# A scan with experts on one core: the copies of a triangular solve at six places, and a transposing matmul three pairs behind its gram

## The chip, the cores and the metric

The kernel runs on one core of one Trainium2 chip. Its metric is the device time of one execution in microseconds (us), the median of several runs. A core has five engines that each work through a queue of their own: TensorE (PE) for matmuls, VectorE (DVE), ScalarE (ACT) and GpSimd (POOL) for elementwise work, and SyncE (SP), which here issues every DMA. PEld is TensorE's weight load.

## The reference, cut to what matters

```python
x = L0_attn_x                                   # (8, 1024, 256)
xn = _layernorm(x, axis=-1)
v = xn @ Wkv[256:].T + bkv[256:]
def step(W, inp):                               # scan over the 1024 time steps
    xt, vt = inp                                # 8 rows, one of each sequence
    y = xt @ W.T
    gW = 2 / (8 * 256) * ((y - vt).T @ xt)
    return W - eta * gW, y
s = scan(step, W0, (xn, v))
probs = softmax(xn @ router_w.T + router_b)     # 16 experts, the best 6, renormalized
ffn = sum over e of (xn @ expert_w[e]) * gate[:, e]   # divided by the gates' sum, plus a tiny term
out = x + s * silu(ffn)
```

The scan is a recurrence: the weight W is corrected after each time step by the error that it made on that step. All else is independent from row to row.

## The kernel before

**Tiles.** The 1024 steps are cut into 64 tiles of 16 steps; a tile has 16 x 8 = 128 rows. Inside a tile the recurrence becomes a triangular system: with A made of the products of the tile's rows with one another (gram), the errors of all 128 rows are the solution of (1 + A) e = p, where p is the error under the W of the tile's start. The kernel inverts the triangle ahead of time, for a batch of tiles at once, and then multiplies. Batches have 1, 1, 2, 4, 4, 4 tiles and then eight each; the batches of eight begin with tiles 16, 24, 32, 40, 48 and 56.

**One tile's steps.** The load of x (L110, on SP), layernorm (L200: bn_stats L204, bn_aggr L206 into mv, xn), a round trip through DRAM that turns xn (bounce L228, xT L230), and the cast of xT into a high and a low part, xT_two (`split`, L151 to L153: ScalarE casts the high part, DVE or POOL subtracts the low one). `products` (L263): two matmuls make gram in PSUM (L268), and ScalarE casts gram's second half, the cross terms, into cross (L274). `products_end` (L276): one matmul against the identity adds cross transposed onto gram (L278), and DVE makes xx (L283) and the masked a (L284). `project` (L286): vr, the values and router logits, from which DVE makes lg and hv. `errors_1` (L524): pe = x W, and p = 2 hv + pe (L534), split into p_hi and p_lo. `errors_2` (L541): the solution e by three matmuls with u_hi and u_lo, from which ScalarE makes step_hi (L546) and DVE step_lo (L548) and hy (L552). `update` (L554): six matmuls add the step to W (wt_ps), and wt_hi and wt_lo are cast from it. `experts` (L566): eight pairs of experts, six matmuls of 128x512 each into h (three PSUM buffers); the parts are scaled by the gates and summed on ScalarE (part, L583), POOL (mix, L586) and DVE (mix, L592 and L594). `finish` (L599): m (L604), th (L606), my (L608, L610, L611) and the output's DMA (L612).

**The solve of a batch** goes through solve_0 to solve_6, on blocks of 32 rows: solve_1 and solve_2 invert the diagonal blocks (q2, then uq at L424, and its transposed form tq at L444). At its end solve_2 copies the four blocks of uq into u_full and the four of tq into t_half, eight copies on ScalarE for a batch of eight (L448, L451). solve_3 makes z (L467 and around), solve_4 y, which is copied into u_full and t_half (L483, L485), solve_5 z2 from u_full (L492, L500), solve_6 y2 from t_half and z2 (L505), and then splits u_full into u_hi and u_lo (L517).

**What sets the order.** PE's and SP's order is the order in which the program text issues the work: `put(slot, pair, what)` (L647) files each step under a tile and a pair of its experts, and the loop at the end (L707 to L715) issues, for each tile and pair, first the steps filed there and then that pair of experts. So one pair of experts, six matmuls of h, is the unit in which steps are placed, eight to a tile. With f the first pair of a batch of eight, its solve_1 to solve_6 stand at f-11, f-9, ... f-1 (L670). Gram of tile i stands at pair 8(i-9)+1 in the long run (L676), products_end one pair later, load 21 pairs ahead of gram, layernorm 10 and transpose_x 1 ahead. The order on ScalarE, DVE and POOL is not written out; a scheduler sets it when the kernel is built, by the text's order as priority and by when it reckons that an instruction's inputs are ready. Gram and vr share two PSUM buffers ("misc").

Of the kernel before, what the change touches and what calls it, by code (L numbers as in the profile page):

```python
# [36 lines left out]
P = 128  # L37
Q = 32
# [5 lines left out]
GROUP = 4  # L44
BATCH = 8
AHEAD = 5
FAR = 9
# [6 lines left out]
def ttt_moe_kernel(  # L54
# [12 lines left out]
    nc = tc.nc  # L67
# [30 lines left out]
    batches = [1, 1, 2, 4, 4, 4]  # L98
# [92 lines left out]
    def at(b, size=Q):  # L191
        return slice(b * size, (b + 1) * size)
# [221 lines left out]
    def step_q(g, name, rhs, out):  # L414

        c = g.count
        ps = solving(f"{name}_ps_{g.n}")
        for j in range(c):
            for b in range(P // Q):
                nc.tensor.matmul(  # L420
                    ps[at(b), j * Q : (j + 1) * Q], lhsT=gram_of(g.first + j)[at(b), 0, at(b)],
                    rhs=rhs[at(b), j, :], start=True, stop=True, skip_group_check=True,
                )
        nc.vector.tensor_add(  # L424
            out, ps[:, : c * Q].rearrange("p (j q) -> p j q", q=Q),
            ident_q.unsqueeze(1).broadcast_to([P, c, Q]),
        )
# [13 lines left out]
    def solve_2(g):  # L441
        c = g.count
        step_q(g, "uq", g.q2, g.uq)
        nc.vector.transpose(  # L444
            g.tq.rearrange("p j q -> p (j q)"), g.uq.rearrange("p j q -> p (j q)")
        )
        for b in range(P // Q):
            nc.scalar.copy(g.u[at(b), :, at(b)], g.uq[at(b)])  # L448
        for odd, js, ms in g.halves:
            for b in range(2):  # L450
                nc.scalar.copy(g.t[at(2 * odd + b), ms, at(b)], g.tq[at(b), js])  # L451

    def solve_3(g):
        c = g.count
# [47 lines left out]
    def solve_6(g):  # L502
# [15 lines left out]
        for j in range(g.count):  # L518
            tiles[g.first + j].u_hi, tiles[g.first + j].u_lo = u_hi[:, j, :], u_lo[:, j, :]

    solve = [solve_1, solve_2, solve_3, solve_4, solve_5, solve_6]


# [93 lines left out]
    opened, started = {}, {}  # L617
# [22 lines left out]

    def solve_x(n, m):
        solve[m](started[n])


    events = {}

    def put(slot, pair, what, *args):  # L647
        events.setdefault((slot, pair), []).append((what, args))
# [19 lines left out]
    for n, c in enumerate(batches):  # L668
        f = 8 * sum(batches[:n])
        spots = solves.get(n, [f - 11 + 2 * m if c > GROUP else f - 10 + 2 * m for m in range(len(solve))])  # L670
        for m, spot in enumerate(spots):
            put(spot // 8, spot % 8, solve_x, n, m)
    preps = {1: 6, 2: 10, 3: 12, 4: 17, 5: 19, 6: 25, 7: 27, 8: 33, 9: 35, 10: 41, 11: 49}
    for i in range(1, NT):
        near = preps.get(i, 8 * (i - AHEAD) + 1)
        spot = preps.get(i, 8 * (i - FAR) + 1)  # L676
        if 11 < i < 23:
            spot = 49 + (i - 11) * 16 // 3
        norm, turn = {1: (1, 4), 2: (7, 9), 3: (8, 8)}.get(i, (spot - 10, spot - 1))
        fetch = max(4, spot - 21)  # L680
        apart = max(turn, 8 * (i - 2) + 6)
        if i >= BY_PE:
            put(fetch // 8, fetch % 8, load, i)
        put(norm // 8, norm % 8, layernorm, i)
        put(turn // 8, turn % 8, transpose_x, i)
        put(apart // 8, apart % 8, split_x, i)
        put(spot // 8, spot % 8, products_x, i)
        put(near // 8, near % 8, project_x, i)
        put((spot + 1) // 8, (spot + 1) % 8, products_y, i)

    ctx.enter_context(tc.manual_schedule(engines={mybir.EngineType.PE, mybir.EngineType.SP}))

# [54 lines left out]
```

## Time and profile before

| what | us |
|---|---|
| median of 3 runs | 1000.82 |
| the three runs | 1002.66, 998.97, 1000.82 |
| the profiled execution's own time | 1001.66 |
| its span, from the first to the last instruction | 999.6 |
| PE busy | 965.9 |
| DVE busy | 763.0 |
| ACT busy | 427.6 |
| POOL busy | 442.1 |

The span is what the hardware profiler saw of one execution; some 2 us of that execution's own time lie around it. Busy times are sums over the span. The rows of groups name the line, the engine, the operation, what is written and read, and the mean time of one; "idle before" is the time in which the engine stood still just ahead of such an instruction, with the instruction that ended most of it. The granted clock of TensorE was 0.997 of full speed. In the plain tiles, the time from the first matmul of a tile's experts to that of the next tile is 14.06 us, and one pair of experts takes 1.4 to 1.6 us of PE.

### The profile page before, as it was taken

The page shows a single profiled execution, that of the slowest core. Times are in us where ns is not written, and L with a number is a line of the kernel's source. Part 1 is how long each engine was busy: PE and PEld are TensorE (multiplying, and loading weights), DVE is VectorE, ACT ScalarE, POOL GpSimd, SP SyncE. Part 2 cuts the span into 40 slices and gives each one's busy share as a digit, 9 for nine tenths or more (in the row PEclk, how much of TensorE's full clock was granted, in tenths as well). Part 3 has the DMA queues.
Part 4 walks back from the last instruction along what each step waited for, and adds up shares of the span by engine and source line. Part 5 has one row for each costly group of instructions (what it writes and reads, how often), then busy time and mean ns, then how long its engine had stood idle before and what let it go on. Part 6 is the DMA issues. An engine that isn't in the chain of part 4 may idle for free.

```text
span 999.6 us, 19616 instructions
## 1 busy us (share of the span) xinstructions
PE 965.9 (97%) x6672; PEld 796.4 (80%) x6672; DVE 763.0 (76%) x2207; ACT 427.6 (43%) x1101; POOL 442.1 (44%) x675
## 2 busy tenths in 40 slices
PE   5999999999999999999999999999999999999997
PEld 4778778878778887888878888788887888888885
DVE  6988696877868878787777878679786787757665
ACT  6654454453443334433344343543335333443332
POOL 6543444444444453444434454344443544343443
PEclk9999999999999999999999999999999999999999
DMA  8111111111111111111110111111110110000000
GB/s 237 30 53 33 48 38 54 42 44 50 26 40 34 34 43 31 36 43 37 27 44 22 43 44 39 27 39 26 42 44 22 43 43 22 8 11 11 11 11 11
DMA packets 67092, 38.66 MB, mean 39 GB/s; under 512 B 38176, under 2 KB 66992, under 8 KB 66992
## 3 DMA queue, kind: packets, MB, share of 16 engines
q1 hardware_dynamic: 66992, 37.41, 13.9%
q8 instruction: 53, 0.87, 0.4%
q14 instruction: 47, 0.39, 0.1%
HBM read 21.13 MB, written 16.25 MB: 37 GB/s over the span
## 4 chain that ended last, share of the span: by engine, by line
PE 53%; DVE 21%; DMA 8%; issue 5%; POOL 5%; ACT 5%; SPq 3%; POOLq 0%; DVEq 0%; ACTq 0%
PE h L259 41%; DVE mix L594 5%; DMA x<-in_L_attn_x_dram 5%; PE pe L259 4%; PE vr L259 3%; ACT part L583 3%; PE wt_ps L259 2%; POOL mix L586 2%; DVE q L433 2%; DMA bounce<-xr 1%; DVE mix L592 1%; DVE wt_lo L153 1%; SPq L230 1%; POOL rstd L210 1%; DMA raw<-in_L_ffn_expert_w_dram 1%
## 5 line engine op out<-in xcount | busy, mean ns | idle before, releaser
L259 PE MATMUL h<-we,xT_two 128*128 128x512 f32 x3072 | 779.7, 399 | 3.7 <-ACT part L583 3.2
L259 PEld LDWEIGHTS h<-we,xT_two 128*128 128x128 f32 x3072 | 554.5, 189 | 119.2 <-ACT part L583 5.8
L594 DVE SCALAR_TENSOR_TENSOR mix<-h,gate,mix 128x256 f32<-128x256 f32 x576 | 265.6, 475 | 87.8 <-PE h L259 52.7
L583 ACT ACTIVATE part<-h,gate 128x256 f32<-128x256 f32 x384 | 182.0, 475 | 315.8 <-DVE mix L594 177.2
L586 POOL TENSOR_TENSOR mix<-mix,part 128x256 f32<-128x256 f32 x256 | 189.6, 741 | 156.6 <-ACT part L583 152.6
L608 POOL TENSOR_TENSOR my<-m,hy 128x256 f32<-128x256 f32 x64 | 47.5, 742 | 167.7 <-DVE m L604 159.9
L611 POOL TENSOR_TENSOR my<-my,x 128x256 f32<-128x256 f32 x63 | 46.5, 738 | 73.1 <-DVE top L387 25.9
L586 POOL TENSOR_TENSOR mix<-part,part 128x256 f32<-128x256 f32 x64 | 48.3, 754 | 50.8 <-ACT part L583 50.8
L152 ACT CAST p_hi<-p 128x256 fp32r<-128x256 f32 x64 | 26.0, 406 | 90.6 <-DVE p L534 90.3
L153 DVE TENSOR_TENSOR wt_lo<-wt_ps,wt_hi 128x512 fp32r<-128x512 f32 x64 | 43.0, 672 | 23.6 <-ACT wt_hi L152 23.6
L259 PE MATMUL vr<-w_vr,xT_two 128*128 128x272 f32 x384 | 60.0, 292 | 0.0
L259 PEld LDWEIGHTS vr<-w_vr,xT_two 128*128 128x128 f32 x384 | 55.7, 191 | 4.3
L204 DVE BATCH_NORM_STATS2 st<-x 128x6 f32<-128x256 f32 x64 | 26.9, 422 | 41.0 <-DMA x<-in_L_attn_x_dram 41.0
L153 POOL TENSOR_TENSOR xn_lo<-xn,xn_hi 128x256 fp32r<-128x256 f32 x64 | 47.7, 746 | 6.5 <-ACT xn_hi L152 6.4
L208 POOL TENSOR_SCALAR ve<-mv 128x1 f32<-128x1 f32 x64 | 15.1, 238 | 78.7 <-DVE mv L206 66.6
L546 ACT ACTIVATE step_hi<-pe,neg_c 128x256 fp32r<-128x256 f32 x64 | 30.3, 474 | 37.0 <-PE pe L259 37.0
L217 DVE TENSOR_SCALAR xn<-x,mv,rstd 128x256 f32<-128x256 f32 x40 | 32.8, 819 | 15.6 <-POOL rstd L210 15.2
L153 DVE TENSOR_TENSOR p_lo<-p,p_hi 128x256 fp32r<-128x256 f32 x64 | 42.5, 664 | 2.5 <-ACT p_hi L152 1.1
L259 PEld LDWEIGHTS pe<-wt_hi,xT_two 128*128 128x128 f32 x256 | 39.0, 188 | 6.0 <-ACT wt_hi L152 0.4
L152 ACT CAST xT_two<-xT 128x256 fp32r<-128x256 f32 x60 | 24.3, 406 | 44.4 <-PE h L259 23.9
L259 PE MATMUL pe<-wt_hi,xT_two 128*128 128x256 f32 x256 | 40.8, 281 | 0.0
L548 DVE SCALAR_TENSOR_TENSOR step_lo<-pe,neg_c,step_hi 128x256 fp32r<-128x256 f32 x64 | 30.4, 475 | 13.5 <-ACT step_hi L546 13.5
(117 smaller groups left out, 1182.8 us busy)
## 6 DMA issues: line engine op xcount, KB each, us to landing
x<-in_L_attn_x_dram SPq DMA_DIRECT2D x64, 128.0 KB, 2.7
out_dram<-my SPq DMA_DIRECT2D x64, 128.0 KB, 2.3
bounce<-xr SPq DMA_DIRECT2D x60, 128.0 KB, 2.3
xT<-bounce SPq DMA_DIRECT2D x240, 32.0 KB, 1.8
raw<-in_L_ffn_expert_w_dram SPq DMA_DIRECT2D x16, 256.0 KB, 6.1
w_raw<-in_L_attn_Wkv_dram SPq DMA_DIRECT2D x1, 256.0 KB, 2.8
w_raw<-in_L_attn_W_dram SPq DMA_DIRECT2D x1, 256.0 KB, 5.6
bias<-in_L_attn_bkv_dram SPq DMA_DIRECT2D x1, 128.0 KB, 4.8
```

Source lines behind the costliest of these rows:

```text
L152: nc.scalar.copy(hi, src)
L153: (engine or nc.vector).tensor_sub(lo, src, hi.bitcast(F32))
L204: nc.vector.bn_stats(st, xt)
L217: nc.vector.tensor_scalar(q.xn, xt, mv[:, 0:1], rstd, ALU.subtract, ALU.mult)
L259: nc.tensor.matmul(o, lhsT=a, rhs=b, start=first and m == 0, stop=(m == len(terms) - 1), **kw)
L546: nc.scalar.mul(q.step_hi, e, neg_c)
L548: nc.vector.scalar_tensor_tensor(q.step_lo, e, neg_c, q.step_hi.bitcast(F32), op0=ALU.mult, op1=ALU.subtract)
L583: nc.scalar.mul(part, he, gate)
L586: nc.gpsimd.tensor_add(new, q.mix[1], part)
L594: nc.vector.scalar_tensor_tensor(new, he, gate, q.mix[j], op0=ALU.mult, op1=ALU.add)
L608: nc.gpsimd.tensor_mul(my, m, q.hy)
L611: (nc.vector if i == NT - 1 else nc.gpsimd).tensor_add(o, o, xt)
```

## The change

There are two edits. First, solve_2 no longer makes the eight copies; a new function `copies(g, lo, hi)` lists them, u's blocks in the order 2, 3, 0, 1 and then t's four, and makes those from lo to hi. For batches of up to four tiles all are issued right behind solve_2, and for batches of eight they are filed as pieces under six pairs: f-8, f-7, f-6 (one u block each), f-5 (two t blocks), f-4 (the last u block), f-3 (two t blocks). Second, gram (`products_x`) of tiles from 23 on is filed two pairs earlier, and with it go the load of x, layernorm and transpose_x, whose places are counted from it; for tiles 12 to 22 the places follow a smaller stride, which is 0 to 2 pairs earlier. The transposing matmul's step (`products_y`) stands three pairs behind gram for tiles from 12 on, instead of one, so that from tile 23 on it stands at the pair where it stood, the third of a tile.

```diff
@@ solve_2
-        for b in range(P // Q):
-            nc.scalar.copy(g.u[at(b), :, at(b)], g.uq[at(b)])
+
+    def copies(g, lo, hi):
+        pieces = [(g.u[at(b), :, at(b)], g.uq[at(b)]) for b in (2, 3, 0, 1)]
         for odd, js, ms in g.halves:
-            for b in range(2):
-                nc.scalar.copy(g.t[at(2 * odd + b), ms, at(b)], g.tq[at(b), js])
+            pieces += [(g.t[at(2 * odd + b), ms, at(b)], g.tq[at(b), js]) for b in range(2)]
+        for to, piece in pieces[lo:hi]:
+            nc.scalar.copy(to, piece)
@@ solve_x
         solve[m](started[n])
+        if m == 1 and batches[n] <= GROUP:
+            copies(started[n], 0, None)
+
+    def copies_x(n, lo, hi):
+        copies(started[n], lo, hi)
@@ the places
+        if c > GROUP:
+            for lo, hi, spot in ((0, 1, f - 8), (1, 2, f - 7), (2, 3, f - 6), (4, 6, f - 5), (3, 4, f - 4), (6, 8, f - 3)):
+                put(spot // 8, spot % 8, copies_x, n, lo, hi)
...
-        spot = preps.get(i, 8 * (i - FAR) + 1)
+        spot = preps.get(i, 8 * (i - FAR) - 1)
         if 11 < i < 23:
-            spot = 49 + (i - 11) * 16 // 3
+            spot = 49 + (i - 11) * 31 // 6
...
-        put((spot + 1) // 8, (spot + 1) % 8, products_y, i)
+        apart = spot + (1 if i < 12 else 3)
+        put(apart // 8, apart % 8, products_y, i)
```

## The prediction

> **What bounds the kernel.** I read the page's head and its chain first, then the list of waits, then the timeline of one tile in which a batch of eight is solved.
>
> ```profile
> span 999.6 us, 19616 instructions
> ...
> PE 965.9 (97%) x6672; PEld 796.4 (80%) x6672; DVE 763.0 (76%) x2207; ACT 427.6 (43%) x1101; POOL 442.1 (44%) x675
> ...
> PE h L259 41%; DVE mix L594 5%; DMA x<-in_L_attn_x_dram 5%; PE pe L259 4%; PE vr L259 3%; ACT part L583 3%; PE wt_ps L259 2%; POOL mix L586 2%; DVE q L433 2%; DMA bounce<-xr 1%; DVE mix L592 1%; DVE wt_lo L153 1%; SPq L230 1%; POOL rstd L210 1%; DMA raw<-in_L_ffn_expert_w_dram 1%
> ```
>
> TensorE (PE) is busy for 97% of the span, so an edit pays only where it takes work from PE (this one takes none) or closes a gap of PE. The starts of the experts' matmuls give each tile's length. A plain tile takes 14.06 us; tiles 15, 23, 31, 39 and 47, in the middle of which a batch of eight is being solved, take 19.5, 19.1, 18.9, 19.7 and 18.9. Most of the excess is the solve's own matmuls. The waits tell what is not:
>
> ```profile
> DVE st L204 <- DMA x<-in_L_attn_x_dram: 41.0, 36, 3.6
> ...
> PEld gram L278 <- ACT cross L274: 11.6, 11, 1.7
> ...
> ACT u_full L448 <- DVE uq L424: 10.6, 8, 1.6
> ...
> PE gram L278 <- DVE hv L296: 6.2, 5, 1.3
> ```
>
> (waiter, releaser, total us, times, longest us.) L278, gram's transposing matmul, needs cross, which ScalarE (ACT) makes at L274. The same gaps show at the weight load and, put down to another releaser, at the matmul, so the rows are not added. From the gaps between PE's instructions I count 1.18 us before L278 in tile 15 and 1.47, 1.48, 1.47 and 1.48 in tiles 23, 31, 39 and 47: 7.08 us. Tiles 10, 13 and 14 add 0.99 + 0.12 + 0.48 = 1.59.
>
> ScalarE in tile 47 (start, duration, engine, line, in brackets the idle time before):
>
> ```profile
> 752.58 1.65 ACT L448 COPY u_full<-uq 32x256 f32<-32x256 f32 x4 [1.56 <-DVE uq L424]
> 754.24 1.22 ACT L451 COPY t_half<-tq 32x128 f32<-32x128 f32 x4
> 755.49 0.41 ACT L152 CAST xT_two<-xT 128x256 fp32r<-128x256 f32 x1
> ...
> 757.61 0.26 ACT L274 CAST cross<-gram 128x128 fp32r<-128x128 f32 x1
> ```
>
> Gram's matmuls are done about 755.2, but the copies (2.9 us) and what queued behind them hold cross back to 757.61. That is the wait aimed at. What else happens in that tile:
>
> ```profile
> 757.55 0.73 POOL L611 TENSOR_TENSOR my<-my,x 128x256 f32<-128x256 f32 x1 [2.29 <-DVE lg L294]
> 758.31 0.59 SPq L612 DMA_DIRECT2D out_dram<-my  x1
> 758.94 0.60 SPq L110 DMA_DIRECT2D x<-in_L_attn_x_dram  x1
> 761.65 0.43 DVE L204 BATCH_NORM_STATS2 st<-x 128x6 f32<-128x256 f32 x1 [2.61 <-DMA x<-in_L_attn_x_dram]
> 762.46 0.45 DVE L548 SCALAR_TENSOR_TENSOR step_lo<-pe,neg_c,step_hi 128x256 fp32r<-128x256 f32 x1
> 762.93 0.72 ACT L483 COPY u_full<-y_ps 32x256 f32<-32x256 f32 x2
> 763.66 0.52 ACT L485 COPY t_half<-y_ps 32x128 f32<-32x128 f32 x2
> 764.33 0.54 PEld L492 LDWEIGHTS z_ps<-u_full,a 64*64 64x64 f32 x16
> ```
>
> This is a second chain, beside the gap. The load of x stands on SyncE (SP) behind the previous tile's output, which waits for POOL. VectorE (DVE), in order, waits 2.61 us for that load at bn_stats, and mix and step_lo queue behind it; ScalarE's next part waits for that DVE mix, and y's copies queue behind that part; z2 (L492) needs the last of them, which ends at 764.18. PE starts z2 at 764.33: the chain has 0.15 us to spare.
>
> **Part 1: the eight copies in six places.** It removes and adds nothing: four copies of 403 ns and four of 297 ns (their rows' means), 2.8 us, per batch of eight. ScalarE's order is not written out by hand, and in the built kernel the eight still stand in one block, in all six batches, ahead of the xT_two and p_hi casts as before; only the order inside u's four is new. A piece placed later in the text was ready as early, and was taken at once. Cost and gain: nothing. If the copies had really been apart, part 1 alone would have let cross through; as built it cannot.
>
> **Part 2: gram at pair 7 of the tile before, L278 still at pair 2.** The two gram matmuls (2 x 0.118 us) and cross (0.261 us) are moved, not added. In the built kernel cross now stands directly ahead of the eight copies. ScalarE idles 1.56 us there, waiting for uq, and that hides the 0.26 us; without that cover the copies, and the chain behind them, would be later by 0.26 in each of six batches, 1.6 us at most. Gram's 0.24 us now comes ahead of the last h of a tile and so delays that tile's last mix, m and p; p_hi is needed by PE at 759.54 and is made at 755.80, so this is covered in the batch tiles. In plain tiles p_hi waits for DVE's p (90.3 us in 49 times, 1.8 us each), and that covers cross as well; uncovered in all of some 40 plain tiles it would be 10 us. I take 0, with ends of -0.1 us (the gap before the two wt_lo matmuls at 751.49, which gram would fill) and +0.26 us a tile.
>
> With cross 1.5 us or more before its use, the waits at L278 go: 7.08 + 1.59 us. **What is late next** is the second chain. The load of x is put two pairs earlier in the text, but on SP it is still issued right behind the same output, and its place on DVE (bn_stats after xx and a, ahead of mix and step_lo) is the same too. The output comes from m, th, my on engines whose order here is unchanged, and these started behind the copies. So in tile 47 bn_stats still starts about 761.65, step_lo ends at 762.91, t_half at 764.18, and z2 can start at 764.25 at the earliest. PE arrives 1.4 us earlier and waits at the update's third matmul or at z2. Gain: 764.33 - 764.25 = 0.08 us instead of 1.48. Tile 31: t_half ends at 523.73, z2 started at 523.80, 0.07. Tiles 15, 23 and 39: z2 already waited for t_half before (0.69, 0.25 and 0.69 us): 0.05 each. In all about **0.3 us of the 7.08**.
>
> The DMA is what this hangs on. Here the load took 2.71 us from issue to use (758.94 to 761.65); the page's median is 2.7. [...]
>
> **Part 3: the early tiles.** For 11 < i < 23 gram, layernorm, the load and the transposition stand 0 to 2 pairs earlier. Here the built order does change: loads of x pass bounces on SP, the bounces of tiles 16, 19 and 22 no longer stand behind an output, the casts of xT_two for tiles 12 and 13 fall behind parts that PE waited for, and tile 12's xx leaves the front of wt_lo. PE's gaps there, apart from L278: tile 5: 0.32 and 0.69 (step_lo); 6: 0.84 (h, released by a part that stood behind xT_two's wait for DMA) and 1.67 (wt_lo); 9: 0.46; 13: 0.21; 14: 0.24 and 0.26: 4.69 us. Each is named by a queue order that changes, but new ones appear: part of tile 8 behind the casts of tiles 17 and 19, wt_hi and part of tiles 10 and 11 behind those of 20 and 22, which may wait for their DMA. The ends are 4.69 gained and the same again lost; I take a third gained, 1.6 us, since the moved casts leave more gaps than they enter. L278's 1.59 us in tiles 10, 13 and 14 I take whole.
>
> **Sum**, against the profiled execution's 1001.66 us (span 999.6 and 2.1 around it): -0.3 - 1.6 - 1.6 = -3.5, 998.2. That execution lay 0.84 above the median of 1000.82, so the forecast is **997.4 us**.
>
> **Rivals.** (a) *The stalls really go.* If the second chain does not bind, because the load lands earlier or the output is out earlier, then 7.08 + 1.59 + 1.6 = 10.3 us go: 991.4, by the median 990.5. For it: PE is the bound at 97%, and every L278 wait is measured. Against: z2's own waits in tiles 15, 23 and 39, and 0.15 us of slack in tile 47. It decides in favour if bn_stats starts over 1 us earlier against the start of its tile. Chance 0.20. (b) *The early queue turns on it, slower.* ScalarE, in order, stands at a cast of xT_two for its DMA while PE needs a part or wt_hi behind it. The row of that wait has 20.2 us in 16 cases, 3.4 the longest; three such new waits at 3.4 that reach PE give +10.2, less 0.3 + 1.6 for what goes anyway: 1010.0, by the median 1009.1. It decides from the point where the bounce and its return (2.3 and 1.8 us, the page's medians) end after ScalarE reaches the cast. Against: in before, the 3.4 us wait cost PE only 0.84. Chance 0.08. (c) *It does not do what it says at all*: copies in one block, L278's wait turned into z2's everywhere, and early gains and losses even: 1000.8, from 999.5 to 1002.5. Chance 0.12. My forecast, 995 to 999.5, has 0.60.
>
> About 0.5%, 5.0 us, is what a measurement of this kernel can tell from no change. Faster by more: (a), 0.20. Within: 0.60 + 0.12 = 0.72. Slower: (b), 0.08. The range takes in (a), the forecast and (c) and leaves out (b): 989.5 to 1002.5.
>
> **What would show it.** Right: the row "gram L278 <- ACT cross" nearly empty; a row for PE waiting at wt_ps (step_lo) or z_ps (t_half) grown to about 1.4 us in each of five tiles; these tiles as long as before within 0.2 us; bn_stats still waiting 2.6 to 3.6 us for x; the eight copies in one stretch. Wrong: tiles 23, 31, 39 and 47 shorter by over 1 us (then the second chain did not bind), or plain tiles over 14.1 us (then cross is not covered).

## The result, and the profile after

The changed kernel takes 1005.91 us (median of six runs, 1004.8 to 1006.83); the kernel before, run beside it, 1000.27 (six runs). The ratio is 1.0055, 95% interval 1.0041 to 1.0069: slower by 0.55%, 5.6 us, where 0.3% faster was forecast.

The head of the page after, and its chain by engine:

```profile
span 1003.8 us, 19608 instructions
...
PE 965.9 (96%) x6672; PEld 798.2 (80%) x6672; DVE 766.9 (76%) x2207; ACT 428.2 (43%) x1101; POOL 441.1 (44%) x675
...
PE 50%; DVE 25%; DMA 8%; issue 5%; ACT 5%; POOL 4%; SPq 2%; POOLq 0%; ACTq 0%; DVEq 0%
```

PE does the same 965.9 us of work, and the span is 4.2 us longer: the chain has 3 points less of PE and 4 more of DVE. The waits of the changed kernel (waiter, releaser, total us, times, longest us):

```profile
DVE st L204 <- DMA x<-in_L_attn_x_dram: 52.1, 38, 3.7
...
PEld h L259 <- ACT part L585: 11.5, 15, 2.4
...
PEld wt_ps L259 <- DVE step_lo L550: 5.4, 5, 1.8
...
PEld z_ps L494 <- ACT t_half L487: 4.8, 7, 0.8
```

No row for L278 waiting for cross is left: 11.6 us have gone. In their place stand five waits of the update (wt_ps) for step_lo, 5.4 us where there were 1.1, z2's for t_half, 4.8 where there were 2.9, and h's for ScalarE's part, 11.5 where there were 5.8.

Tile 23 of the changed kernel, all engines (start, duration, engine, line; lines behind L444 have moved: the copies are L453, step_lo is L550, z2 L494):

```profile
392.71 0.28 ACT L274 CAST cross<-gram 128x128 fp32r<-128x128 f32 x1
394.39 1.65 ACT L453 COPY u_full<-uq 32x256 f32<-32x256 f32 x4 [1.40 <-DVE uq L424]
396.05 1.22 ACT L453 COPY t_half<-tq 32x128 f32<-32x128 f32 x4
...
400.13 0.59 SPq L614 DMA_DIRECT2D out_dram<-my  x1
400.76 0.60 SPq L110 DMA_DIRECT2D x<-in_L_attn_x_dram  x1
404.51 0.43 DVE L204 BATCH_NORM_STATS2 st<-x 128x6 f32<-128x256 f32 x1 [3.69 <-DMA x<-in_L_attn_x_dram]
405.33 0.45 DVE L550 SCALAR_TENSOR_TENSOR step_lo<-pe,neg_c,step_hi 128x256 fp32r<-128x256 f32 x1
406.51 0.52 ACT L487 COPY t_half<-y_ps 32x128 f32<-32x128 f32 x2
```

The eight copies stand in one block, as before, with cross ahead of them. The second chain is there too, whole: output, load of x behind it, bn_stats 3.69 us in wait for that load, then step_lo and t_half. PE arrives earlier and waits at step_lo and t_half.

Which tiles became longer, summed from the starts of the experts' matmuls in each profile (us); the rows e1 to e12 are the experiments below:

| kernel | from the start to the end of tile 4 | tiles 5-14 | 15, 23, 31, 39, 47 | 18, 26, 34, 42, 50 | 22, 30, 38, 46, 54 | other | tile 63 |
|---|---|---|---|---|---|---|---|
| before | 110.8 | 159.4 | 96.2 | 72.8 | 80.4 | 461.8 | 18.2 |
| change | 111.4 | 161.0 | 98.5 | 73.6 | 79.4 | 461.6 | 18.2 |
| e1 copies alone | 110.3 | 159.5 | 95.7 | 72.7 | 80.0 | 461.8 | 18.2 |
| e2 steady part alone | 110.5 | 159.9 | 100.3 | 74.1 | 79.9 | 461.6 | 18.2 |
| e3 early part alone | 110.8 | 161.3 | 95.4 | 72.6 | 80.6 | 461.8 | 18.2 |
| e4 change, load moved | 110.8 | 160.5 | 97.3 | 74.1 | 80.1 | 462.1 | 18.2 |
| e5 steady part, filler | 111.1 | 161.9 | 97.6 | 74.9 | 80.1 | 461.6 | 18.2 |
| e6 change, queue moved | 111.7 | 161.2 | 87.7 | 73.0 | 81.2 | 461.7 | 18.2 |
| e7 steady part, queue moved | 110.6 | 161.0 | 87.9 | 73.1 | 82.7 | 461.7 | 18.2 |
| e8 before, queue moved | 110.7 | 160.3 | 97.7 | 74.4 | 83.8 | 466.0 | 18.2 |
| e9 change, output on POOL | 119.4 | 152.4 | 88.4 | 73.1 | 80.2 | 462.1 | 21.7 |
| e10 before, output on POOL | 119.6 | 152.4 | 87.3 | 70.4 | 79.2 | 462.5 | 21.7 |
| e11 before, POOL from tile 4 | 111.9 | 155.6 | 87.5 | 70.4 | 79.1 | 462.4 | 19.6 |
| e12 change, POOL from tile 4 | 111.5 | 156.1 | 89.0 | 72.9 | 79.9 | 462.2 | 19.6 |

The plain tiles are as they were. The change loses 2.3 us in the five tiles it was made for, 1.6 in tiles 5 to 14 and 0.8 in the third tile of each batch (18 to 50), and gains 1.1 in tiles 22 to 54. (The first tiles differ by up to 1.4 us between kernels that are the same there.)

Tile 15 shows something that no wait explains. Its two waits together are shorter than the three of before, 0.88 us for step_lo and 0.68 for t_half against 1.18 (cross), 0.18 (step_lo) and 0.69 (t_half), and yet the tile is 0.98 us longer. The windows of that tile (start:end, length; busy us and instructions of PE, PEld, DVE, ACT and POOL; granted clock; DMA):

```profile
279.10:282.50 3.40, 3.40 (x53) 2.81 (x43) 0.62 (x3) 0.53 (x2) 0.73 (x1) 1.00 0.40 118
282.50:285.90 3.40, 2.16 (x25) 1.61 (x24) 2.97 (x9) 1.71 (x6) 1.48 (x3) 1.00 0.17 39
285.90:289.40 3.50, 3.50 (x10) 2.71 (x9) 1.46 (x3) 2.35 (x6) 2.48 (x4) 0.51 0.02 5
289.40:292.80 3.40, 3.40 (x32) 2.69 (x31) 1.48 (x3) 2.16 (x6) 0.41 (x1) 1.00 0.00 0
```

In the second window PE is busy for 2.16 of 3.40 us, since both waits lie in it. In the third the granted clock is a half: each 128x512 matmul takes 0.43 us from start to start instead of 0.23, eight of them, 1.5 us lost. Then it is full again. Tile 39 has the same spell, after 647.7 us. In the profile of before the clock is full from 24 us to the last matmuls.

### The profile page after: what moved, and what is told of

It reads as the page before. It is cut to its first block, busy times and chain, and to the rows that moved or that the text cites. A ratio compares the mean times of both kernels' runs of the same rounds, so it can differ in the third digit from the quotient of the medians.

```text
span 1003.8 us, 19608 instructions
## 1 busy us (share of the span) xinstructions
PE 965.9 (96%) x6672; PEld 798.2 (80%) x6672; DVE 766.9 (76%) x2207; ACT 428.2 (43%) x1101; POOL 441.1 (44%) x675
## 4 chain that ended last, share of the span: by engine, by line
PE 50%; DVE 25%; DMA 8%; issue 5%; ACT 5%; POOL 4%; SPq 2%; POOLq 0%; ACTq 0%; DVEq 0%
PE h L259 39%; DVE mix L596 5%; DMA x<-in_L_attn_x_dram 5%; PE pe L259 4%; PE vr L259 3%; ACT part L585 2%; DVE q L433 2%; PE wt_ps L259 2%; DMA bounce<-xr 2%; DVE mix L594 1%; POOL mix L588 1%; DVE xn L217 1%; DVE wt_lo L153 1%; DVE a L284 1%; POOL my L613 1%
## 5 line engine op out<-in xcount | busy, mean ns | idle before, releaser
L259 PEld LDWEIGHTS h<-we,xT_two 128*128 128x128 f32 x3072 | 554.3, 189 | 121.6 <-ACT part L585 11.5
L613 POOL TENSOR_TENSOR my<-my,x 128x256 f32<-128x256 f32 x63 | 46.7, 741 | 74.4 <-DVE top L387 31.6
L550 DVE SCALAR_TENSOR_TENSOR step_lo<-pe,neg_c,step_hi 128x256 fp32r<-128x256 f32 x64 | 30.5, 477 | 13.4 <-ACT step_hi L548 13.4
L259 PE MATMUL wt_ps<-step_lo,xn_hi 128*128 128x256 f32 x126 | 36.1, 286 | 4.4 <-DVE step_lo L550 4.4
```

What stands on the lines that cost most here:

```text
L259: nc.tensor.matmul(o, lhsT=a, rhs=b, start=first and m == 0, stop=(m == len(terms) - 1), **kw)
L550: nc.vector.scalar_tensor_tensor(q.step_lo, e, neg_c, q.step_hi.bitcast(F32), op0=ALU.mult, op1=ALU.subtract)
L613: (nc.vector if i == NT - 1 else nc.gpsimd).tensor_add(o, o, xt)
```

## The experiments

All ratios are to the kernel before, run on the same chip beside the kernel.

**e1: the copies alone.** Gram and all else as before; the diff of `solve_2` and its six places is the change's own.

> Of the change only the first edit: the eight copies filed under six pairs, gram and all else where it stood. My theory: nothing, a ratio to before of 0.998 to 1.002, the waits of L278 for cross at 11 to 12 us as before, because the built order is that of before apart from the order of u's blocks. Rival: the copies do cost something (their new order, or the code's layout), and part of the +0.55% is theirs: 1.002 or more.

Measured: 0.9997 (0.9988 to 1.0006). The first edit does nothing: on each engine the built order is that of before, but for the order of u's four blocks.

**e2: the steady part of the second edit alone.**

```diff
-        spot = preps.get(i, 8 * (i - FAR) + 1)
+        spot = preps.get(i, 8 * (i - FAR) - (1 if i >= 23 else -1))
...
-        put((spot + 1) // 8, (spot + 1) % 8, products_y, i)
+        apart = spot + (1 if i < 23 else 3)
+        put(apart // 8, apart % 8, products_y, i)
```

> Of the change only the steady part of the second edit: for tiles from 23 on gram two pairs earlier and L278 at its old pair; the copies and tiles 12 to 22 as before. My theory: L278's wait goes, and PE waits instead at step_lo and at t_half within 2 us of each other, 1.4 to 2.4 us a tile in tiles 15, 23, 31, 39, 47; in one to three of these TensorE's clock falls to half for 3.4 us, 1.7 us lost each time. Net -1 to +5 us, ratio 0.999 to 1.005, and tiles 10 and 11 as before. Rival: the two moved steps cost nothing by themselves and the loss lies in the early tiles alone: L278's gain shows, ratio 0.993 to 0.997.

Measured: 1.0034 (1.0019 to 1.0048), and in its profile three spells of half clock, in tiles 23, 31 and 47, each right behind the two waits. Over its six runs the mean granted clock is 0.9930; in the 22 runs of before of the same batch it is 0.9973. A mean clock lower by 0.0043 over 1004 us is up to 4.3 us of full speed, enough for the whole loss of 3.4.

**e3: the early part alone.**

```diff
-            spot = 49 + (i - 11) * 16 // 3
+            spot = 49 + (i - 11) * 31 // 6
...
-        put((spot + 1) // 8, (spot + 1) % 8, products_y, i)
+        apart = spot + (3 if 11 < i < 23 else 1)
+        put(apart // 8, apart % 8, products_y, i)
```

> Of the change only the early part of the second edit: tiles 12 to 22 with the smaller stride, and L278 three pairs behind their gram; the copies and the tiles from 23 on as before. My theory: tiles 10 and 11 grow by 3.3 us together (part and wt_hi late, behind DVE's transposition waiting for the bounce), tiles 5 to 9 and 12 to 14 shrink by 1.7: ratio 1.001 to 1.003, and the clock stays at full from 25 us on. Rival: the early tiles' difference was that one execution's, and the loss is all in the steady part: 0.998 to 1.0005.

Measured: 1.0018 (1.0009 to 1.0027), and the mean clock is that of before (0.9975). Tiles 5 to 14 are 1.8 us longer: tiles 5 and 6 give 1.7, tiles 10 and 11 take 3.6. What holds them, in the changed kernel's tiles 10 and 11 (DVE, ACT and SP; in e3 such rows come some 0.2 us earlier):

```profile
201.84 0.45 DVE L223 STREAM_TRANSPOSE xr<-xn 128x256 f32<-128x256 f32 x1 [1.50 <-DMA bounce<-xr]
202.75 1.07 ACT L585 ACTIVATE part<-h,gate 128x256 f32<-128x256 f32 x2 [2.92 <-DVE total L405]
...
212.53 0.60 SPq L614 DMA_DIRECT2D out_dram<-my  x1
213.23 1.47 SPq L228 DMA_DIRECT2D bounce<-xr  x1
216.08 0.45 DVE L223 STREAM_TRANSPOSE xr<-xn 128x256 f32<-128x256 f32 x1 [3.05 <-DMA bounce<-xr]
217.89 0.55 SPq L110 DMA_DIRECT2D x<-in_L_attn_x_dram  x1
220.46 0.43 DVE L204 BATCH_NORM_STATS2 st<-x 128x6 f32<-128x256 f32 x1 [2.46 <-DMA x<-in_L_attn_x_dram]
```

There is one buffer xr. Its next transposition waits until the bounce has read it, the bounce stands on SP behind an output, and DVE, in order, stands for 1.5 and 3.05 us with the gates and mixes behind it that ScalarE's parts need. The first of these waits reaches PE in tile 10: h stands 1.4 us for the part at 202.75, and pe then 0.65 us for wt_hi. The second opens no gap of PE by itself. Tile 11 loses its 1.2 us only at 226.20, at a part that stands on ScalarE behind xn; xn waits for DVE, which had by then stood another 2.46 us at bn_stats for the load issued at 217.89, behind that bounce and its return. In the kernel before the same wait is 1.67 us in tile 11, and there is none in tile 10.

Together: e2's and e3's excesses, 0.34 and 0.18%, add up to 0.52 of the change's 0.55%.

**e4: the change, with the load ahead of the output on SP.** The reading so far puts the loss on bn_stats, in wait for a load behind an output.

```diff
-        fetch = max(4, spot - 21)
+        fetch = max(4, spot - (21 if i < 23 else 23))
```

> The change, and the loads of x for tiles from 23 on filed two pairs earlier again, so that on SP each stands ahead of the output instead of behind it. My theory: bn_stats no longer waits in tiles 15, 23, 31, 39 and 47, so the waits for step_lo and t_half there (7.1 us) go, and with them the spells of half clock (2 x 1.7): ratio to before 0.993 to 0.998, about 10 us under the change. Rival: these waits come from elsewhere (y's copies, POOL's output chain), and 1.003 to 1.007 stays.

Measured: 1.0039 (1.0027 to 1.0052). A miss. The scheduler answered with another order on DVE; tile 47:

```profile
763.71 0.45 DVE L223 STREAM_TRANSPOSE xr<-xn 128x256 f32<-128x256 f32 x1 [2.02 <-DMA bounce<-xr]
764.08 0.44 DVE L596 SCALAR_TENSOR_TENSOR mix<-h,gate,mix 128x256 f32<-128x256 f32 x1
764.44 0.47 DVE L550 SCALAR_TENSOR_TENSOR step_lo<-pe,neg_c,step_hi 128x256 fp32r<-128x256 f32 x1
```

Now xr's transposition stands where bn_stats stood, waits 2.02 us for the bounce behind the same output, and mix and step_lo wait behind it. Over the kernel that wait grew from 5.0 (the change) to 36.6 us. It is not the load alone: whatever layernorm step the scheduler puts there waits for SP's queue. Nor is it the clock: e4's profile has no spell and its five runs a mean clock of 0.9968, and yet its ratio is at least 1.0027.

**e5: PE kept busy in the two waits.** The kernel of e2, with 128x256 matmuls, in a new function fill, that compute nothing the output needs; no wait is taken away, and 7.7 us of PE work are added (5 x 13 x 0.118).

```diff
     def update(i):
...
+        if i % 8 == 7 and 8 < i < 48:
+            q.filler = misc(f"filler_{i}")
+            fill(i, 8)
...
+        if i % 8 == 7 and 8 < i < 48:
+            fill(i, 5)
         wt = new_state(i + 1)
```

> The kernel of the steady part alone (gram two pairs earlier for tiles from 23 on), with matmuls that compute nothing in the two waits of tiles 15, 23, 31, 39 and 47: eight of 128x256 ahead of the update and five between it and z2, 0.118 us each, into a spare PSUM tile that nobody reads. They add work to PE and take no wait away. My theory: the spells of half clock follow from PE being idle twice within 3.4 us, so they go, the granted clock from 25 us on stays at 1.00, the waits for step_lo and t_half shrink by what the filler fills, and the time falls by 1.7 us a spell: ratio 0.999 to 1.002, against 1.0034 without filler. Rival: the spells have another cause (the load, chance), and the ratio stays at 1.003 or rises to 1.006 by the added work.

Measured: 1.0016 (1.0006 to 1.0026), with more work than e2. No spell in its profile, and the mean clock over twelve runs is 0.9968, close to the 0.9973 of before. The five tiles take 97.6 us instead of 100.3. The intervals of e2 and e5 overlap, so the time alone does not separate them; the clock does. On ScalarE, DVE and POOL the two built orders are the same, so nothing but the filler and the PSUM buffer that it takes differs.

**e6: the change, with loads two tiles earlier and layernorm five pairs earlier.**

```diff
-        fetch = max(4, spot - 21)
+        fetch = max(4, spot - 21) if i < 24 else max(91, spot - 37)
...
-        norm, turn = {1: (1, 4), 2: (7, 9), 3: (8, 8)}.get(i, (spot - 10, spot - 1))
+        norm, turn = {1: (1, 4), 2: (7, 9), 3: (8, 8)}.get(i, (spot - (10 if i < 25 else 15), spot - 1))
```

> The change, with the loads of x for tiles from 24 on filed two tiles earlier and layernorm for tiles from 25 on five pairs earlier, so that bounces stand ahead of the output on SP and each load has landed long before its bn_stats. My theory: neither bn_stats nor xr waits for DMA in tiles 15 to 47 any more, step_lo and t_half come in time, L278's gain shows at last (7 us less than the change) and the half clock goes: ratio 0.993 to 0.997. Rival: another wait takes the place again (y's copies, DVE's own work), and it stays above 1.000.

Measured: 0.9926 (0.9909 to 0.9943), and all five tiles at 17.4 to 18.2 us. But not for the reason given. Tile 47 of this kernel (DVE, ACT, PE):

```profile
754.88 0.48 DVE L596 SCALAR_TENSOR_TENSOR mix<-h,gate,mix 128x256 f32<-128x256 f32 x1
757.59 0.43 DVE L204 BATCH_NORM_STATS2 st<-x 128x6 f32<-128x256 f32 x1 [2.23 <-DMA x<-in_L_attn_x_dram]
757.93 0.47 DVE L550 SCALAR_TENSOR_TENSOR step_lo<-pe,neg_c,step_hi 128x256 fp32r<-128x256 f32 x1
...
755.45 0.47 ACT L585 ACTIVATE part<-h,gate 128x256 f32<-128x256 f32 x1
755.82 0.72 ACT L485 COPY u_full<-y_ps 32x256 f32<-32x256 f32 x2
756.55 0.52 ACT L487 COPY t_half<-y_ps 32x128 f32<-32x128 f32 x2
...
759.25 0.68 PE L494 MATMUL z_ps<-u_full,a 64*64 64x64 f32 x16
```

bn_stats still waits 2.23 us for its load. What is different is what stands behind it: that mix is now ahead, so ScalarE's part and y's copies come at once, t_half is done at 757.07, 2.2 us before PE wants z2, and step_lo ends at 758.40, in time for PE. In these tiles the wait at bn_stats was not itself the loss; what queued behind it on DVE was.

**e7: the steady part of the change with that queue, early tiles and copies as before** (e2 with e6's two edits).

> As the run before, but with tiles 12 to 22 placed as in the kernel before, and the copies too: the steady part of the change with the queue cleared. My theory: the 1.8 us that the early part costs are saved as well: ratio 0.991 to 0.996, the fastest so far. Rival: early and steady part depend on one another, and it is no faster than that run.

Measured: 0.9934 (0.9919 to 0.9949), not apart from e6. The 1.8 us of the early part were not saved here: tiles 5 to 14 take 161.0 us, as in the change.

**e8: the kernel before with that queue** (e6's two edits alone).

> The kernel before with the loads and layernorm moved in the same way, and nothing of the change. My theory: L278 still waits 7 us in the five tiles, since cross is still behind the copies; only z2's waits go: ratio 0.997 to 1.000. Rival: it is the queue that costs time and not L278, and this is as fast as the run with gram moved: 0.991 to 0.996.

Measured: 1.0102 (1.0086 to 1.0117), 18 us over e6. Outside both expectations:

```profile
DVE xr L223 <- DMA bounce<-xr: 29.4, 28, 2.8
...
PEld gram L278 <- ACT cross L274: 19.5, 24, 1.9
```

L278 waits for cross 24 times instead of 11, in plain tiles too (20, 21, 28, 29, 37, 44, 45, 49). The same two edits that let the change win make the kernel before lose. Under this queue the change is worth 1.8% (1.0102 to 0.9926); under the old one it costs 0.55%.

**e9 and e10: the outputs issued from POOL,** where the addition that they wait for is made, so that no load or bounce stands behind them. e9 is the change, e10 the kernel before.

```diff
-        nc.sync.dma_start(
+        nc.gpsimd.dma_start(
             out=out[:, i * TS : (i + 1) * TS, :].rearrange("b t d -> t b d"), in_=o
```

> The change, with the outputs' DMA issued from POOL, right behind the addition that they wait for, instead of from SP. SP's queue then holds only loads, bounces and their return. My theory: the early tiles and the tiles 15 to 47 share one cause, loads and bounces standing on SP behind an output that waits for POOL, so both losses go: the waits of bn_stats and xr for DMA nearly empty, tiles 15 to 47 at 17.3 to 18 us, tiles 5 to 14 at or under the 159.4 us of before, ratio 0.989 to 0.995. Rival: a DMA issued from POOL holds up POOL's additions, or the early loss has another cause: 0.996 or more.

> The kernel before with the outputs' DMA issued from POOL and nothing of the change. My theory, after the last run of this kind: without gram's move L278 still waits for cross behind the copies, 7 us, and more where ScalarE is filled earlier: ratio 1.000 to 1.010. Rival: that run's loss came from layernorm's new place, and with SP free this one gains as the change does: 0.990 to 0.997.

Measured: e9 0.9965 (0.9952 to 0.9978), e10 0.9905 (0.9891 to 0.992). Tiles 5 to 14 fall to 152.4 us in both, by 8.7 and 7.0, which ties the early loss to SP's queue; part of this may be the delay in tile 1, which lets the other engines get ahead (in e11 and e12, without it, these tiles take 155.6 and 156.1). Against my expectation it is the kernel without the change that gains more, and the range given for e9 was too good. Both pay 6 to 7 us in tile 1 and 3.6 in tile 63.

**e11 and e12: the same, from tile 4 on and not for the last.**

```diff
+        (nc.gpsimd if 3 < i < NT - 1 else nc.sync).dma_start(
```

> The kernel before, with the outputs of tiles 4 to 62 issued from POOL and those of tiles 0 to 3 and 63 from SP. My theory: the 6.8 us that the outputs on POOL cost in tile 1 and the 3.6 in tile 63 go, the gain in tiles 5 to 54 stays, and no wait at L278 is left without any move of gram: ratio 0.978 to 0.985, the fastest. Rival: the first DMA from POOL costs the 6 us wherever it comes, and the ratio stays at 0.987 to 0.991.

> The change with the same queues as the run before. My theory: where SP's queue no longer delays the loads, the wait that the change aims at does not exist, and what is left of the change is its cost, 0.3 to 0.8% over the run before: ratio 0.982 to 0.992. Rival: gram's earlier place pays once the start is undisturbed, and this is as fast as the run before or faster.

Measured: e11 0.9837 (0.9823 to 0.9852), 987.4 us against 1003.58, the fastest of all; e12 0.9893 (0.9876 to 0.9911). Tile 1's cost is gone, so it belonged to the first outputs on POOL; of tile 63's 3.6 us, 1.4 are left. e11's waits:

```profile
DVE st L204 <- DMA x<-in_L_attn_x_dram: 37.3, 27, 3.4
...
PEld gram L278 <- ACT cross L274: 0.3, 1, 0.3
```

L278 hardly waits at all, though gram, L278 and the copies stand where they stood in the kernel before. Tile 39 of the kernel before, which starts at 631.30 (ACT, DVE):

```profile
629.61 0.58 ACT L152 CAST wt_hi<-wt_ps 128x512 fp32r<-128x512 f32 x1
...
631.61 0.41 DVE L424 TENSOR_TENSOR uq<-uq_ps,ident_q 128x256 f32<-128x256 f32 x1
```

The same tile of e11, which starts at 620.81 (DVE, ACT, PE):

```profile
617.65 0.58 ACT L152 CAST wt_hi<-wt_ps 128x512 fp32r<-128x512 f32 x1
...
619.98 0.42 DVE L424 TENSOR_TENSOR uq<-uq_ps,ident_q 128x256 f32<-128x256 f32 x1
...
620.43 1.65 ACT L448 COPY u_full<-uq 32x256 f32<-32x256 f32 x4 [1.89 <-DVE uq L424]
622.42 1.22 ACT L451 COPY t_half<-tq 32x128 f32<-32x128 f32 x4
624.90 0.26 ACT L274 CAST cross<-gram 128x128 fp32r<-128x128 f32 x1
...
625.41 0.22 PE L278 MATMUL gram<-ident_r,cross 128*128 128x128 f32 x1
```

uq starts 0.83 us ahead of the tile's start, where it came 0.31 us behind it in the kernel before, and ScalarE's wt_hi comes 3.2 us before that start instead of 1.7: the engines no longer enter the tile late. The copies are as long as ever and nearly as far ahead of cross (4.5 us from the first to cross, 5.0 before), and cross ends 0.25 us before L278 wants it. So the eight copies alone were not enough to make L278 wait. In its text e11 differs from the kernel before in the outputs' queue only, so the rest of that wait went with it. But the scheduler also built another order (278 of DVE's 2207 instructions and 109 of POOL's 675 don't fit into the order of before), and no run has the one without the other.

What the change still costs there, 0.9893 against 0.9837, is not the clock (mean 0.9970 and 0.9955). Two rows that grew from e11 to e12, as they are in e12 (in e11 4.5 us in 10 cases and 5.2 in 6):

```profile
ACT cross L274 <- PE gram L268: 15.5, 29, 1.3
...
PEld h L259 <- ACT part L585: 8.8, 12, 2.4
```

ScalarE now reaches cross before gram is made, but that is not where PE's longest gaps come from. From tile 15 on they are waits of h for part in tiles 15, 31 and 47 (0.9, 0.45 and 0.5 us), behind a mix that stands on DVE behind bn_stats in wait for its load (2.42, 1.54 and 2.05 us), and in tiles 26 and 34 (0.8 and 0.35), behind DVE's q and r_den. These gaps are about half of what e12 is slower; the rest is open, and no run tested this reading.

## Why the prediction was wrong, point by point

- *Part 1, the copies: nothing.* Right (e1, 0.9997), and for the reason given: a piece placed later in the text was ready as early and was taken at once.
- *Cross ahead of the copies and in the plain tiles: nothing.* Right: the plain tiles take 14.06 us as before, and "other" in the table is 461.6 against 461.8.
- *L278's waits go, and step_lo and t_half wait in their place; 0.3 us are left of 7.08.* Right in mechanism. The five tiles together are 2.3 us longer, not 0.3 shorter; without the 3.0 us of the two spells they would be 0.7 shorter. Tiles 31 and 47 are 0.15 and 0.18 us shorter, near the 0.07 and 0.08 foreseen. But the load, on which the chain hangs, was taken to last as long as before: in tile 23 it is in use 3.75 us after its issue instead of 2.95, and that tile is 0.75 us longer without a spell, while in tiles 15 and 39 it comes 0.8 and 0.6 us sooner.
- *The first step that failed, in part 2: the exchange of one wait for another was priced by its length alone, with nothing for where the new wait stands.* In before, L278's wait and z2's lie over 6 us apart; after, step_lo's and t_half's lie within 1.5 us, and in two of the five tiles of the profile PE's clock drops, 1.5 us each. The mean clock of the change's six runs is 0.9942, against 0.9973 for before in the runs beside e1 to e4: at most 3.1 us of 1004, over half of the loss. None of the rivals had it.
- *The second step that failed, part 3, the early tiles: 4.69 us gained or lost, a third gained, and L278's 1.59 whole: 3.2 us gained.* Wrong in sign. e3 lost 1.8 in these tiles. The hazard was named on the wrong engine: rival (b) had ScalarE at a cast in wait for its DMA, and it was DVE at xr in wait for the bounce. The ends given, 4.69 gained or lost, hold it; the value taken between them does not.
- *Rival (a), the second chain does not bind.* It bound. But its condition, bn_stats earlier, was not the right one: e6 gained with bn_stats in wait as ever, and e11 with 37.3 us of such waits against 41.0. The condition is what stands behind bn_stats on DVE when PE comes.
- *The range, 989.5 to 1002.5.* It ended at "nothing gained"; both costs lay beyond it.

The split, from the two profiles, whose spans lie some 4.2 us apart: 3.0 by the clock, 1.6 in the early tiles, 0.8 in the third tiles (h waiting for part) and 0.6 up to the end of tile 4, less 0.7 in the five tiles, 1.1 in tiles 22 to 54 and 0.2 elsewhere. The medians lie 5.6 apart because the profiled execution of before took 1.4 us more than the median of its runs and that of the change 0.4 less. What stays open: why the earlier places of layernorm and of the loads cost the kernel before 10 us (e8), which was seen in the waits and not taken apart.

## What to carry to other kernels

A wait at a busy engine can be the last sign of lateness that comes from elsewhere: ask first why the releaser was late. Here one output, waiting at the head of SP's queue, held the loads and bounces behind it (in tile 23 of the changed kernel the load was issued 0.04 us after the output's issue had ended, and bn_stats stood 3.69 us for it), these held DVE, and DVE held everybody; moving that one DMA to the queue of the engine that makes its data was worth 1.6% (e11, with the order that the scheduler then built), while hiding the symptom cost 0.55%. And price a moved wait by its neighbours: in the changed kernel two gaps of PE that came within 1.5 us of each other had half clock behind them in two of five tiles, 1.5 us lost each time on top of the gaps.

## What the runs showed of the hardware

The two spells of half clock in the changed kernel's profile last 3.41 us each (285.93 to 289.35 and 647.75 to 651.16 us); in them the 128x512 matmuls come every 0.43 us, elsewhere every 0.23. Neither PE's busy share nor the length of the waits tells the tiles with a spell from those without one. In the 3.41 us in front of these two spells PE was busy for 2.17 and 1.97 us. In the kernel before it was busy for 1.91 of the 3.41 us from 140.82 on, and the clock stayed at 1.00. The two waits in front of the spells were 0.9 and 0.7 us in tile 15 and 1.1 and 0.7 in tile 39; in tile 23, where the clock stayed at 1.00, they were 1.8 and 0.7, and PE was busy for 1.26 of the 3.42 us from 403.67 on. What sets off a spell was not shown.

The output's DMA from POOL took 2.3 us to land, the same as from SP (the pages of e11 and before). e11's outputs landed no sooner; its loads and bounces did, in 2.5 us instead of 2.7 and 1.7 instead of 2.3 by the medians, and no run tells that part of the gain from the freed queue.
